# Last stage of a four-stage transformer kernel: the experts' choice compared through DRAM in place of TensorE products, and three moves of VectorE work

## The chip, the cores and the metric

The kernel runs on one core of a Trainium2 chip. The core has TensorE (matmuls), VectorE (elementwise work, reductions, 32x32 transposes), ScalarE (activation functions), GpSimd (called POOL in the profile) and SyncE (SP), which here issues nearly all DMAs. The engines run their own instruction streams and wait for each other through semaphores. The metric is the device time of the whole program in microseconds; lower is better. All data are float32.

## The reference, cut to what matters

Four residual blocks follow one another on x of shape (16, 256, 256). The change is in the fourth, a gated linear attention (GLA) with a dense branch and four sparse experts:

```
q1, k1, v = x @ Wq, x @ Wk, x @ Wv                    # 8 heads of 64
q2 = x @ Wqa @ Wqb
k2 = softmax(x @ Wka @ Wkb) over each head
gk1, gk2 = log_sigmoid(x @ Wg?a @ Wg?b + bg?) / 16
e = softmax(x @ We)                                    # 4 experts per token
mask = one_hot(top_1(e)); rw = e * mask
o_dense  = chunk_gla(q1, k1, v, gk1)
o_sparse = sum over experts of chunk_gla(q2 * rw, k2 * rw, v, gk2 * mask)
o = rmsnorm(o_dense + o_sparse) * silu(x @ Wga @ Wgb)
out = x + tanh(g) * (o @ Wo)
```

Since each token has one expert, the sum over experts needs two things only for every pair of tokens (s, t): whether they chose the same expert, and, if so, the product of their two weights. The first masks the cumulated gates, the second masks the scores of the sparse branch.

## The kernel before, in words

The program has four stages. The last one, `stage3_fast` (line 1619), is a generator: its first parts, for batch 0, run between parts of stage 2, then its own loop runs over p = 0 to 63: 16 batches of four steps, each step one pair of heads (m = p % 4). Batch 0 is prepared ahead of the loop; inside the loop, the preparation of batch b + 1 is spread over the four steps of batch b.

The order is written out by hand. The objects `dve3`, `act3` and `pool3`, and the wrappers `matmul` and `transpose`, keep program order on their engine, so each engine works through its instructions exactly in the order in which the loop calls the functions. What happens once a batch hangs in small tables (`start`, `middle`, `rest`, `late`, `behind_mask`, `by_rows`, `logs`, lines 2036 to 2045), each a point within the step; `{1: [(route, 1)]}` means: in the second step of a batch, do `route` for the next batch. I call p % 4 = 0, 1, 2, 3 the first to fourth step.

One step p does, in this order: `masked(p - 1, 1)` (scores of the sparse branch times the masks, on VectorE, out of the two-bank PSUM tile `sc`; POOL then adds both branches in `at`); `keys_queries(p + 1)` (tile `kq`); `decays(p + 1)` (matmuls of the gates with the masks, tiles `gq` and `gz`, the second with `em`, and ScalarE's exponentials `ee`); `products(p, 0)` and `masked(p, 0)`; `factors(p + 1)` (`f`); the values of the step before, tile `o`; `second` and `factors_second` (`k`, `q`); `products(p, 1)`. There is one `sc` tile, so each set of products waits until VectorE has read the set before. Small PSUM results share two banks, given out by `bank`.

Work once a batch that the change and the prediction touch:

- `lows` (1695, first step): low-rank projections, tile `low`; the four expert logits are four of its rows, so tokens lie along the free dimension.
- `route_rows` (1712), called from `products` in the first step: two TensorE transposes bring the logits to 128 token partitions.
- `route_logits` (1718), `route_sums` (1732), `route` (1737): softmax, maximum, first maximum on 128x2x4 tiles; the result is the one-hot row times its weight, tile `hot`.
- `turn_hot` (1782), `turned_hot` (1788): two TensorE transposes and a copy give `hT`, 4 experts x 256 tokens. `pairs` (1792): two matmuls of `hT` with itself, tile `both`, give for each pair the product of the weights, zero where the experts differ. VectorE makes `em` (a zero or one pattern times the causal mask) and `am` (the product times the score mask).
- `steepest` (1778): a maximum over the gates for the final range check, 128x1024, twice.
- `all_gates` (1758, second step): gate projections; two of its four results go into the `sc` tile, two into small banks.
- `outgates` (1811, first step): output gate into two small banks; ScalarE takes an exponential `eg` of each, VectorE copies each to `zs`. `outgates_end` (1825): logarithm and exponential, then POOL multiplies to `gw`.
- `turn_ahead` (1685, third step, behind `masked`): VectorE transposes the 32x32 blocks of the normalised rows of batch b + 2, 16 DMAs of 16 KB put the blocks in place (`xnT<-turned`).
- `norms` (1985, second step): ScalarE writes 8 KB to DRAM (`rms<-rs`), and two DMAs read it back spread over 64 partitions each (`r<-rms`).

SyncE issues its DMAs in order too, and a DMA that waits holds up those behind it.

Of the kernel before, what the change touches and what calls it, by code (L numbers as in the profile page):

```python
# [17 lines left out]
P = 128  # L18
# [55 lines left out]
def layers(ctx: ExitStack, tc: tile.TileContext, t, out, check):  # L74
# [1544 lines left out]
    def stage3_fast(early_bank):  # L1619

        with ExitStack() as sx:
# [29 lines left out]
            hots = [w1.tile([P, 2, 4], F32, tag=f"hot{n}", name=f"hot{n}") for n in range(2)]  # L1651
# [43 lines left out]
            def lows(b):  # L1695
# [8 lines left out]
                dve3.tensor_scalar(low[b][:, 1, :], ps[:, S:], vec[:, V_ONE:V_ONE + 1], None, ALU.add)  # L1704
                lowd[b] = of(b).tile([P, S], F32, tag="lowd", name="lowd")
# [4 lines left out]
            e_, den_, z_ = {}, {}, {}  # L1710

            def route_rows(b, ps):

                for i in range(2):
                    transpose(ps[:, 64 * i:64 * i + 64], low[b][64:P, 1, tokens(i)], ident[64:P, 64:P])
                z_["rt"] = ps

            def route_logits(b):

                ps = z_.pop("rt")  # L1720
                src = ps.rearrange("p (i e) -> p i e", i=2)[:, :, 17:21]
                mx = st.tile([P, 2], F32, tag="emx", name="emx")
                dve.tensor_reduce(mx, src, AX.X, ALU.max)
                e = e_[b] = st.tile([P, 2, 4], F32, tag="e", name="e")
                dve.tensor_tensor(e, src, bc(mx, [P, 2, 4], 2), ALU.subtract)
                act.activation(e, e, AF.Exp)

            def route_first(b):
                route_rows(b, bank("rt")[:, :P])
                route_logits(b)  # L1730

            def route_sums(b):
                den = den_[b] = st.tile([P, 2], F32, tag="eden", name="eden")
                dve.tensor_reduce(den, e_[b], AX.X, ALU.add)
                dve.reciprocal(den, den)

            def route(b):
                e, shape = e_.pop(b), [P, 2, 4]
                dve.tensor_tensor(e, e, bc(den_.pop(b), shape, 2), ALU.mult)
                m, q, c = (st.tile(x, F32, tag=n, name=n) for n, x in (("em", [P, 2]), ("eq", shape), ("ec", [P, 2])))  # L1740
                dve.tensor_reduce(m, e, AX.X, ALU.max)
                first = bc(prio[:, 4:], shape, 1)
                dve.tensor_tensor(q, e, bc(m, shape, 2), ALU.is_equal)
                dve.tensor_tensor(q, q, first, ALU.mult)
                dve.tensor_reduce(c, q, AX.X, ALU.max)
                dve.tensor_tensor(q, q, bc(c, shape, 2), ALU.is_equal)
                dve.tensor_tensor(hots[b % 2], q, e, ALU.mult)
# [34 lines left out]
            def turn_hot(b):  # L1782
                ps = bank("hT")
                for i in range(2):
                    transpose(ps[:4, tokens(i)], hots[b % 2][:, i, :], ident)
                z_[b, "hot"] = ps

            def turned_hot(b):
                hT[b] = of(b).tile([4, S], F32, tag="hT", name="hT")
                dve3.tensor_copy(hT[b], z_.pop((b, "hot"))[:4, :S])  # L1790

            def pairs(b):

                x, both = hT.pop(b), bank("both")
                matmul(both[:, 0:S], x[:, :P], x, start=True, stop=True)
                matmul(both[:, S:3 * P], x[:, P:], x[:, P:], start=True, stop=True)
                em[b] = of(b).tile([P, 2, P], F32, tag="em", name="em")
                dve3.scalar_tensor_tensor(em[b], both.rearrange("p (i s) -> p i s", i=2)[:, :, :P], 0.0, dmask,
                                          ALU.is_gt, ALU.mult)
                am[b] = of(b).tile([P, 384], F32, tag="am", name="am")  # L1800
                dve3.tensor_tensor(am[b], both[:, :384], amask, ALU.mult)
# [9 lines left out]
            def outgates(b):  # L1811
# [7 lines left out]
                for h, ps in enumerate(two):  # L1819
                    e, zs = (w2.tile([P, 512], F32, tag=n, name=n) for n in ("eg", "zs"))  # L1820
                    act3.activation(e, ps, AF.Exp, scale=-1.0)
                    dve3.tensor_copy(zs, ps)
                    z_[b, h] = zs, e
# [82 lines left out]
            def products(p, n):  # L1906
# [4 lines left out]
                if n == 0 and m == 0 and b + 1 < B:  # L1911
                    route_rows(b + 1, ps[:, 1, 384:])
# [121 lines left out]


            start = {3: [(pairs, 1)]}
            middle = {0: [(lows, 1)], 1: [(all_gates, 1)], 2: [(turn_hot, 1)], 3: [(scaled_first, 0)]}

            rest = {0: [(bias, 2)], 2: [(turned_hot, 1), (norm_ahead, 2)], 3: [(steepest, 1, 0), (steepest, 1, 1)]}
            late = {1: [(norms, -1)], 2: [(vals, 1)], 3: [(project, -1)]}  # L2040
            behind_mask = {0: [(route_logits, 1)], 2: [(turn_ahead, 2)]}
            by_rows = {0: [(outgates, 0)], 1: [(gates_end, 1)]}
            logs = {0: [(route_sums, 1), (outgates_end, 0, 0)],
# [11 lines left out]
            for group in (((bias, 0), (stats, 0)), ((norm, 0),), ((turn, 0),), ((lows, 0),), ((gates, 0, 0),),  # L2055
                          ((gate_logs, 0, 0), (route_first, 0)), ((route_sums, 0), (gates, 0, 1)),
# [6 lines left out]
            for f, *a in ((turn_hot, 0), (turned_hot, 0), (stats, 1), (pairs, 0), (norm, 1), (steepest, 0, 0),  # L2063
                          (steepest, 0, 1)):
                f(*a)
# [185 lines left out]
```

## Time and profile before

| | us |
|---|---|
| median of 3 runs (lowest, highest) | 1831.25 (1830.49, 1833.01) |
| the profiled execution: time, span from first to last instruction | 1833.27, 1831.5 |
| TensorE busy (PE), weight loads (PEld) | 1793.7 (98%), 1242.3 (68%) |
| VectorE (DVE), ScalarE (ACT), GpSimd (POOL) busy | 1137.3 (62%), 832.2 (45%), 1015.0 (55%) |
| first instruction of the last stage for batch 0 on TensorE (`low`) | at 1201.6 |

The profile names a group of instructions by engine, line, operation and out<-in of the program's tiles. Nearly all instructions of the last stage stand at a few lines, those of the helpers (L50 for VectorE, ScalarE and POOL, L1637 for matmuls, L1640 for transposes), so the tile names tell them apart. A wait is put down to what released it: "PE sc <- DVE at" is TensorE waiting, before it writes `sc`, for VectorE's instruction that writes `at`.

### The profile page before, as it was taken

Reading aid. Unit: us, or ns where it says so; the run is one execution under the profiler, and the core shown is the slowest. Engines: PE = TensorE matmul, PEld = TensorE weight load, DVE = VectorE, ACT = ScalarE, POOL = GpSimd, SP = SyncE. Lnnn points to the kernel's source line nnn. Section 1 sums busy time; section 2 is a strip of 40 time slices with the busy share of each in tenths; the row PEclk is TensorE's granted clock in tenths of the full one; section 3 lists DMA queues with packets and bytes.
Section 4 is the critical chain, followed back from the end, with each engine's and each line's share of the span. In section 5 each row is a group of like instructions: output and inputs, shape, how many; then the busy total and the mean of one; then the engine's idle time right before and its main releaser. Section 6 shows DMA issues by size and latency. Waiting matters only on the chain.

```text
span 1831.5 us, 35425 instructions
## 1 busy us (share of the span) xinstructions
PE 1793.7 (98%) x13930; PEld 1242.3 (68%) x13930; DVE 1137.3 (62%) x2695; ACT 832.2 (45%) x1727; POOL 1015.0 (55%) x1001
## 2 busy tenths in 40 slices
PE   8999999999999999999999999998999999999997
PEld 5666666666666666666777866656777777777775
DVE  3345656666656666666475388866666666666664
ACT  4433335343443334534343388754544454445432
POOL 3654766567666677656643866313454445444533
PEclk9999999999999999999999999999999999999999
DMA  9800010000010100000067933100111111111110
GB/s 303 231 1 22 16 35 13 28 17 16 31 35 10 30 20 10 28 24 17 13 207 244 256 64 50 24 3 11 35 30 36 29 31 34 34 31 27 38 31 26
DMA packets 110361, 98.05 MB, mean 54 GB/s; under 512 B 43835, under 2 KB 97763, under 8 KB 109673
## 3 DMA queue, kind: packets, MB, share of 16 engines
q1 hardware_dynamic: 97897, 78.91, 14.5%
q0 software_dynamic: 12288, 16.79, 4.5%
q8 instruction: 112, 1.84, 0.4%
q14 instruction: 64, 0.52, 0.1%
HBM read 52.03 MB, written 38.41 MB: 49 GB/s over the span
## 4 chain that ended last, share of the span: by engine, by line
PE 81%; DVE 7%; POOL 7%; ACT 2%; issue 2%; DMA 1%; SPq 0%; POOLq 0%; DVEq 0%; ACTq 0%
PE o L50 12%; PE qk L50 11%; PE v L50 9%; PE sc L50 8%; PE proj L50 7%; PE sc L1637 5%; PE kq L1637 5%; POOL es L50 4%; PE gq L1637 3%; PE v L1637 3%; PE proj L1637 3%; PE ex L50 3%; DVE at L50 2%; PE o L1637 2%; POOL rs L50 2%
## 5 line engine op out<-in xcount | busy, mean ns | idle before, releaser
L50 POOL TENSOR_SCALAR rs<-mv 128x2 f32<-128x2 f32 (+2 forms) x85 | 16.3, 191 | 398.3 <-DVE mv L50 396.5
L50 DVE RECIPROCAL rd<-o 128x256 f32<-128x256 f32 x64 | 112.3, 1755 | 155.9 <-PE o L50 155.9
L50 ACT ACTIVATE e<-sc 128x1024 f32<-128x1024 f32 (+1 forms) x192 | 181.6, 1016 | 18.4 <-PE sc L50 18.4
L50 POOL TENSOR_TENSOR at<-at,at 128x768 f32<-128x768 f32 x63 | 114.2, 1812 | 133.5 <-DVE at L50 133.5
L50 PE MATMUL sc<-qk 64*128 64x256 f32 (+1 forms) x1536 | 183.1, 384 | 0.5 <-DVE qk L50 0.5
L50 PE MATMUL o<-e,v 128*32 128x256 f32 (+1 forms) x3072 | 177.9, 379 | 0.0
L50 PEld LDWEIGHTS sc<-qk 64*128 64x128 f32 (+1 forms) x1536 | 132.0, 172 | 55.1 <-issue 26.8
L50 POOL TENSOR_TENSOR esum<-esum,es 128x512 f32<-128x512 f32 x128 | 163.4, 1277 | 10.0
L50 PE MATMUL qk<-kvT,wkv 128*128 128x333 f32 x512 | 164.3, 443 | 0.0
L50 POOL TENSOR_TENSOR es<-e 128x1024 f32<-128x1024 f32 x64 | 151.3, 2364 | 12.0 <-ACT e L50 9.0
L50 ACT ACTIVATE qk<-qk 128x256 f32<-128x256 f32 x128 | 48.8, 382 | 231.7 <-PE qk L50 231.7
L50 POOL TENSOR_TENSOR es<-es,e 77x1024 f32<-77x1024 f32 x64 | 150.3, 2349 | 5.0
L50 DVE TENSOR_TENSOR at<-sc,amask 128x768 f32<-128x768 f32 x64 | 61.3, 958 | 135.1 <-PE sc L1637 79.6
L50 PEld LDWEIGHTS o<-e,v 128*32 128x32 f32 (+1 forms) x3072 | 99.9, 110 | 66.2
L50 PE MATMUL qk<-kvT,wq 128*128 128x256 f32 x512 | 134.6, 385 | 0.0
L50 DVE COPY qk<-qk 128x333 f32<-128x333 f32 x128 | 64.6, 505 | 94.8 <-ACT qk L50 93.3
L50 POOL DMA_INDIRECT x<-rows_out,pos x64 | 100.9, 1577 | 35.8 <-issue 18.7
L50 PEld LDWEIGHTS qk<-kvT,wq 128*128 128x128 f32 x512 | 94.3, 189 | 35.1 <-issue 9.6
L50 PEld LDWEIGHTS qk<-kvT,wkv 128*128 128x128 f32 x512 | 97.2, 190 | 30.0
L50 PE MATMUL proj<-wo0h,oT 128*128 128x256 f32 x512 | 113.7, 380 | 0.3 <-DVE oT L50 0.3
L50 PE MATMUL v<-wkv,kvT 128*128 128x512 f32 x256 | 113.1, 595 | 0.0
L50 PEld LDWEIGHTS proj<-wo0h,oT 128*128 128x128 f32 x512 | 95.9, 190 | 13.9 <-issue 0.8
(267 smaller groups left out, 3919.5 us busy)
## 6 DMA issues: line engine op xcount, KB each, us to landing
rows<-zero SPq DMA_DIRECT2D x16, 640.0 KB
xin<-rows SPq DMA_DIRECT2D x16, 640.0 KB
r<-rms SPq DMA_DIRECT2D x30, 256.0 KB
rows_out<-y SPq DMA_DIRECT2D x16, 384.0 KB
v<-vctx SPq DMA_DIRECT2D x15, 308.0 KB
x<-in_x_dram SPq DMA_DIRECT2D x16, 256.0 KB
rows_out<-y SPq DMA_DIRECT2D x16, 256.0 KB
out_dram<-x SPq DMA_DIRECT2D x15, 256.0 KB
```

The lines of the kernel that those rows point to most:

```text
L50: x = getattr(self.engine, name)(*a, **k)
L1637: tc.keep_in_program_order(nc.tensor.matmul(*a, **k))
```

## The change

The experts' choice no longer goes through TensorE.

- `lows` gains a VectorE transpose of 32 rows x 256 tokens, so that the logits lie on 32 partitions, 8 blocks of tokens, 4 experts. `route_rows`, `route_first`, `turn_hot`, `turned_hot` and `pairs` are gone. `route_logits` and `route_sums` do the same arithmetic on 32 partitions with 8x4 values each.
- `route` ends with the weight `w` and the priority number `c` of the chosen expert, one of each per token, in the tile `choice`, a 32x32 transpose to `chosen`, and three DMAs on SyncE: 2 KB to DRAM (`picks`), that read back to all 128 partitions (`rows`, 256 KB, in a buffer of the tag `zs`, or for batch 0 of the tag `xn`), and read back with the tokens on the partitions (`cols_`, 128x2x2, in single 4-byte values).
- `same` (fourth step, first thing) makes `em` by comparing rows with columns, one instruction per half. `weights` (fourth step, behind `steepest`) makes `am` with four instructions: compare and multiply by the row weight, then multiply by the column weight and the mask.
- `outgates` takes the exponential and the VectorE copy of the first bank only; the second bank's exponential and copy, by `outgates_exp`, come later in the step, and the copy is made by ScalarE.
- `route_sums` moves from the end of the first step to behind `masked(p - 1, 1)` in the second.
- `turn_ahead` moves from behind `masked(p, 0)` of the third step to ahead of it, behind `vals`.
- Before the loop, batch 0 gets `steepest`, then `same` and `weights`, then `norm(1)`.

```diff
@@ -1648,7 +1648,8 @@
             low2 = w1.tile([64, P], F32, tag="low2", name="low2")
             wo = w1.tile([P, 4, D], F32, tag="wo", name="wo")
 
-            hots = [w1.tile([P, 2, 4], F32, tag=f"hot{n}", name=f"hot{n}") for n in range(2)]
+            choice, chosen = (w1.tile([P, 32], F32, tag=n, name=n) for n in ("choice", "chosen"))
+            nc.gpsimd.memset(choice, 0.0)
 
             xn, xnT, low, lg, hT, em, am, lowd = {}, {}, {}, {}, {}, {}, {}, {}
             v, gw, u_, oT = {}, {}, {}, {}
@@ -1702,49 +1703,50 @@
                                          start=k == 0, stop=k == 1)
                 dve3.tensor_copy(low[b][:, 0, :], ps[:, :S])
                 dve3.tensor_scalar(low[b][:, 1, :], ps[:, S:], vec[:, V_ONE:V_ONE + 1], None, ALU.add)
+                rl[b] = w1.tile([P, 4, P], F32, tag="turned", name="rl")[:, :2, :].rearrange("p x d -> p (x d)")
+                dve3.transpose(rl[b][64:96, :], ps[64:96, S:])
                 lowd[b] = of(b).tile([P, S], F32, tag="lowd", name="lowd")
                 nc.sync.dma_start(out=lowd[b][64:], in_=low[b][:64, 1, :])
                 if b > 0:
                     nc.sync.dma_start(out=low2, in_=low[b][64:, 1, P:])
 
-            e_, den_, z_ = {}, {}, {}
-
-            def route_rows(b, ps):
-
-                for i in range(2):
-                    transpose(ps[:, 64 * i:64 * i + 64], low[b][64:P, 1, tokens(i)], ident[64:P, 64:P])
-                z_["rt"] = ps
+            e_, den_, z_, rl, rows, cols_ = {}, {}, {}, {}, {}, {}
+            picks = [tc.dram_tile([2, S], F32, name=f"picks{b}") for b in range(B)]
+            few, own_rows = [32, 8, 4], slice(64, 96)
+
+            def small(name, shape):
+                return w1.tile([P] + shape[1:], F32, tag=name, name=name)[own_rows]
 
             def route_logits(b):
 
-                ps = z_.pop("rt")
-                src = ps.rearrange("p (i e) -> p i e", i=2)[:, :, 17:21]
-                mx = st.tile([P, 2], F32, tag="emx", name="emx")
+                src = rl.pop(b)[own_rows].rearrange("p (k c) -> p k c", c=32)[:, :, 17:21]
+                mx = small("emx", few[:2])
                 dve.tensor_reduce(mx, src, AX.X, ALU.max)
-                e = e_[b] = st.tile([P, 2, 4], F32, tag="e", name="e")
-                dve.tensor_tensor(e, src, bc(mx, [P, 2, 4], 2), ALU.subtract)
+                e = e_[b] = small("e", few)
+                dve.tensor_tensor(e, src, bc(mx, few, 2), ALU.subtract)
                 act.activation(e, e, AF.Exp)
 
-            def route_first(b):
-                route_rows(b, bank("rt")[:, :P])
-                route_logits(b)
-
             def route_sums(b):
-                den = den_[b] = st.tile([P, 2], F32, tag="eden", name="eden")
+                den = den_[b] = small("eden", few[:2])
                 dve.tensor_reduce(den, e_[b], AX.X, ALU.add)
                 dve.reciprocal(den, den)
 
             def route(b):
-                e, shape = e_.pop(b), [P, 2, 4]
-                dve.tensor_tensor(e, e, bc(den_.pop(b), shape, 2), ALU.mult)
-                m, q, c = (st.tile(x, F32, tag=n, name=n) for n, x in (("em", [P, 2]), ("eq", shape), ("ec", [P, 2])))
-                dve.tensor_reduce(m, e, AX.X, ALU.max)
-                first = bc(prio[:, 4:], shape, 1)
-                dve.tensor_tensor(q, e, bc(m, shape, 2), ALU.is_equal)
-                dve.tensor_tensor(q, q, first, ALU.mult)
+
+                e, q = e_.pop(b), small("eq", few)
+                w, c = choice[own_rows, :8], choice[own_rows, 8:16]
+                dve.tensor_tensor(e, e, bc(den_.pop(b), few, 2), ALU.mult)
+                dve.tensor_reduce(w, e, AX.X, ALU.max)
+                dve.tensor_tensor(q, e, bc(w, few, 2), ALU.is_equal)
+                dve.tensor_tensor(q, q, bc(prio[own_rows, 4:], few, 1), ALU.mult)
                 dve.tensor_reduce(c, q, AX.X, ALU.max)
-                dve.tensor_tensor(q, q, bc(c, shape, 2), ALU.is_equal)
-                dve.tensor_tensor(hots[b % 2], q, e, ALU.mult)
+                dve.transpose(chosen[own_rows], choice[own_rows])
+                nc.sync.dma_start(out=picks[b].rearrange("n (k a) -> (n k) a", a=32), in_=chosen[64:80])
+                x = w2.tile([P, 512], F32, tag="zs", name="rows") if b else w0.tile([P, 2, D], F32, tag="xn", name="rows")
+                rows[b] = x.rearrange("p (n s) -> p n s", n=2) if b else x
+                nc.sync.dma_start(out=rows[b], in_=bc(picks[b], [P, 2, S], 0))
+                cols_[b] = w1.tile([P, 2, 2], F32, tag="cols", name="cols")
+                nc.sync.dma_start(out=cols_[b], in_=picks[b].rearrange("n (i p) -> p n i", p=P))
 
             def gates(b, i):
 
@@ -1779,26 +1781,22 @@
                 dve3.tensor_reduce(check["gates"][:, 2 * b + i:2 * b + i + 1],
                                         lg[b][:, i].rearrange("p n f -> p (n f)"), AX.X, ALU.max)
 
-            def turn_hot(b):
-                ps = bank("hT")
+            def same(b):
+
+                em[b] = of(b).tile([P, 2, P], F32, tag="em", name="em")
                 for i in range(2):
-                    transpose(ps[:4, tokens(i)], hots[b % 2][:, i, :], ident)
-                z_[b, "hot"] = ps
-
-            def turned_hot(b):
-                hT[b] = of(b).tile([4, S], F32, tag="hT", name="hT")
-                dve3.tensor_copy(hT[b], z_.pop((b, "hot"))[:4, :S])
-
-            def pairs(b):
-
-                x, both = hT.pop(b), bank("both")
-                matmul(both[:, 0:S], x[:, :P], x, start=True, stop=True)
-                matmul(both[:, S:3 * P], x[:, P:], x[:, P:], start=True, stop=True)
-                em[b] = of(b).tile([P, 2, P], F32, tag="em", name="em")
-                dve3.scalar_tensor_tensor(em[b], both.rearrange("p (i s) -> p i s", i=2)[:, :, :P], 0.0, dmask,
-                                          ALU.is_gt, ALU.mult)
-                am[b] = of(b).tile([P, 384], F32, tag="am", name="am")
-                dve3.tensor_tensor(am[b], both[:, :384], amask, ALU.mult)
+                    dve3.scalar_tensor_tensor(em[b][:, i, :], rows[b][:, 1, tokens(i)], cols_[b][:, 1, i:i + 1],
+                                               dmask[:, i, :], ALU.is_equal, ALU.mult)
+
+            def weights(b):
+
+                w, c = (rows[b][:, n, :] for n in range(2))
+                x = am[b] = of(b).tile([P, 384], F32, tag="am", name="am")
+                for i, (lo, hi) in enumerate(((0, S), (S, 3 * P))):
+                    dve3.scalar_tensor_tensor(x[:, lo:hi], c[:, i * P:], cols_[b][:, 1, i:i + 1], w[:, i * P:],
+                                               ALU.is_equal, ALU.mult)
+                    dve3.scalar_tensor_tensor(x[:, lo:hi], x[:, lo:hi], cols_[b][:, 0, i:i + 1], amask[:, lo:hi],
+                                               ALU.mult, ALU.mult)
 
             def vals(b):
                 v[b] = of(b).tile([P, 2, 512], F32, tag="v", name="v")
@@ -1818,9 +1816,14 @@
                         matmul(two[h][:, i * S:(i + 1) * S], w[:, m * P:(m + 1) * P], x, start=True, stop=True)
                 for h, ps in enumerate(two):
                     e, zs = (w2.tile([P, 512], F32, tag=n, name=n) for n in ("eg", "zs"))
-                    act3.activation(e, ps, AF.Exp, scale=-1.0)
-                    dve3.tensor_copy(zs, ps)
-                    z_[b, h] = zs, e
+                    z_[b, h] = zs, e, ps
+                outgates_exp(b, 0, dve3.tensor_copy)
+
+            def outgates_exp(b, h, copy):
+                zs, e, ps = z_[b, h]
+                act3.activation(e, ps, AF.Exp, scale=-1.0)
+                copy(zs, ps)
+                z_[b, h] = zs, e
 
             def outgates_end(b, h):
                 zs, e = z_.pop((b, h))
@@ -1908,8 +1911,6 @@
                 b, m, cols = place(p)
                 q, k = fq.pop((p, n)), fk.pop((p, n))
                 ps = psa.tile([P, 2, 512], F32, tag="sc", name="sc")
-                if n == 0 and m == 0 and b + 1 < B:
-                    route_rows(b + 1, ps[:, 1, 384:])
                 for lo, hi, i in ((0, S, 0), (P, S, 1)):
                     for j in range(2):
                         r = slice(64 * j, 64 * j + 64)
@@ -2033,14 +2034,14 @@
                     matmul(ps, ones, v[B - 1][:, 0, :], start=True, stop=True)
 
 
-            start = {3: [(pairs, 1)]}
-            middle = {0: [(lows, 1)], 1: [(all_gates, 1)], 2: [(turn_hot, 1)], 3: [(scaled_first, 0)]}
-
-            rest = {0: [(bias, 2)], 2: [(turned_hot, 1), (norm_ahead, 2)], 3: [(steepest, 1, 0), (steepest, 1, 1)]}
-            late = {1: [(norms, -1)], 2: [(vals, 1)], 3: [(project, -1)]}
-            behind_mask = {0: [(route_logits, 1)], 2: [(turn_ahead, 2)]}
+            start = {3: [(same, 1)]}
+            middle = {0: [(lows, 1)], 1: [(all_gates, 1)], 3: [(scaled_first, 0)]}
+
+            rest = {0: [(bias, 2)], 1: [(route_sums, 1)], 2: [(norm_ahead, 2)], 3: [(steepest, 1, 0), (steepest, 1, 1), (weights, 1)]}
+            late = {1: [(norms, -1)], 2: [(vals, 1), (turn_ahead, 2)], 3: [(project, -1)]}
+            behind_mask = {0: [(route_logits, 1)]}
             by_rows = {0: [(outgates, 0)], 1: [(gates_end, 1)]}
-            logs = {0: [(route_sums, 1), (outgates_end, 0, 0)],
+            logs = {0: [(outgates_exp, 0, 1, act3.copy), (outgates_end, 0, 0)],
                     1: [(route, 1), (stats, 2), (outgates_end, 0, 1), (gate_logs, 1, 0)],
                     2: [(gate_logs, 1, 1), (normed_out, -1, 0), (normed_out, -1, 1)]}
 
@@ -2053,15 +2054,14 @@
                 x.tied = True
             yield
             for group in (((bias, 0), (stats, 0)), ((norm, 0),), ((turn, 0),), ((lows, 0),), ((gates, 0, 0),),
-                          ((gate_logs, 0, 0), (route_first, 0)), ((route_sums, 0), (gates, 0, 1)),
+                          ((gate_logs, 0, 0), (route_logits, 0)), ((route_sums, 0), (gates, 0, 1)),
                           ((route, 0), (vals, 0), (gate_logs, 0, 1), (bias, 1))):
                 for f, *a in group:
                     f(*a)
                 yield
             psu = sx.enter_context(tc.tile_pool(name="f3psu", bufs=1, space=PSUM, side="right", reuse_waits="tile"))
             keys_queries(0)
-            for f, *a in ((turn_hot, 0), (turned_hot, 0), (stats, 1), (pairs, 0), (norm, 1), (steepest, 0, 0),
-                          (steepest, 0, 1)):
+            for f, *a in ((stats, 1), (steepest, 0, 0), (steepest, 0, 1), (same, 0), (weights, 0), (norm, 1)):
                 f(*a)
             yield
             w1 = sx.enter_context(tc.tile_pool(name="f3w1", bufs=1, reuse_waits="tile"))
```

## The prediction

> **What bounds the kernel now.** The change lies in the last stage, so I first cut the span into windows of 37 us, about one batch of that stage, then read who waits for whom in it, then the chain of waits inside one batch. A line of the windows view gives start:end and length, busy us (and instructions) of PE, PEld, DVE, ACT, POOL, then clock, DMA share and GB/s:
>
> ```profile
> 1499.00:1536.00 37.00, 36.53 (x254) 26.89 (x252) 24.25 (x60) 17.75 (x43) 17.68 (x18) 1.00 0.13 32
> ```
>
> TensorE is busy 36.5 of 37 us at full clock; VectorE, the next, 24.3. Every window from 1277 to 1758 reads alike, so the stage runs at the pace of TensorE. Two views say what else it spends. The waits of PE over the stage (total, times, longest):
>
> ```profile
> PE sc L1637 <- DVE at L50: 7.7, 16, 1.0
> PE low L1637 <- DMA xnT<-turned: 1.7, 1, 1.7
> PE sc L1637 <- ACT lg L50: 0.6, 1, 0.6
> PE o L1637 <- POOL at L50: 0.5, 1, 0.5
> ```
>
> and the chain of waits through one batch (start, us, what):
>
> ```profile
> 1509.62 0.22 PE hT L1640 x2
> ...
> 1517.11 0.84 PE both L1637 x4
> ...
> 1532.30 0.28 PE sc L1640
> ...
> 1535.44 1.29 DVE zs L50 x2
> 1536.73 0.33 DVE q L50
> 1537.06 0.08 DVE eden L50
> 1537.14 0.02 issue
> 1537.16 0.17 DVE eden L50
> 1537.33 1.30 DVE at L50 x4
> 1538.63 0.04 issue
> 1538.67 0.70 PE sc L1637 x2
> ```
>
> The batch repeats every 36.76 us (1501.91, then 1538.67). The last lines are the one place where TensorE stands still in each batch: `all_gates` takes the score bank that `masked` reads, and waits 0.46 us for it.
>
> **TensorE work removed**, in 15 of 16 batches (batch 0 is prepared before the loop). `turn_hot`: 0.22 us by the chain, and its neighbours follow without a gap. `pairs`: 0.84; the check is that from the first score matmul before it to the next `kq` is 1.60 us here and 0.75 one step earlier, where nothing stands between. `route_rows`: the chain says 0.28, but from the end of the matmuls before to the start of those behind the scores is 0.78 us with it and 0.78 and 0.79 in the third and fourth steps without it. Its two 64-column transposes seem to run in half of the array beside the scores, so it is worth between 0 and 0.28; I take 0.1, near the equal intervals. Sum 1.16 us, times 15 = **17.4 us**.
>
> **The 0.46 us wait.** Ahead of the four `at` instructions that release the bank, VectorE loses the second gate copy (1.29 us for two, so 0.64) and `route_sums` (q to at, 0.27): it is ready 0.91 us earlier, while TensorE arrives only 0.1 earlier. VectorE's added 0.44 us transpose in `lows` (row: the 128x256 transpose `dens`, 439 ns) falls between 1532.25 and the scores at 1533.3, where it idles 1.21 us. What is late next: the second gate bank, now freed by ScalarE. Its order becomes Exp, Square 0.60, Exp 0.38, Exp 0.58, copy (row: `v` copy, 592 ns); from 1534.9 that ends near 1537.5, and TensorE wants the bank at 1538.15. The wait goes: 14 x 0.45 + 1.0 (the first) = **7.3 us**. The price is on POOL: ScalarE's Ln and Exp (1.28) end near 1538.8, not 1537.83, so `gw` (1.27) and the sum of `at` (1.81) end at 1541.9, and TensorE now reaches the values at 1541.8: 0.1 a batch, **1.5 us back**; between 0 and 0.5 a batch, as the ScalarE order packs. Moved `route_sums` lies in 3.28 us of VectorE idle behind the masking.
>
> **VectorE in the fourth step of a batch** is the tightest place. Gone: `em` 0.425, `am` 0.547, and the 0.70 transpose of `turn_ahead`, which moves one step of the order up into 3.78 us of idle before 1515.14. So q ends at 1517.03, not 1517.63. Added: two 128-column selections (row: `at<-sc,kden,am`, 341 ns at 128 columns, 472 at 256; in a row they cost 0.08 less each) 0.6 us; four in `weights` 2 x 0.47 + 2 x 0.34 = 1.6. Line: selections to 1517.58, at to 1518.88, gating to 1519.48, the two maxima (2.33) to 1521.73, weights to 1523.3. The projection, without the 0.84 of `pairs`, is ready at 1523.43. It fits with 0.1 us to spare, so cost 0; SBUF operands could make the six shorter, dependent pairs longer, and 0.5 us over would be 7 us in all. `route` has six small instructions of 0.16 to 0.2 us for seven. In the first batch no projection covers the masks, so VectorE runs late there: about 2.0 us lost, and against it the only wait for xnT, 1.7 + 0.2 us with its weight load, goes because the turned rows leave 3.5 us sooner. Net 0.1.
>
> **The new transfers.** The added wait is `same`, for rows and cols; behind it on VectorE stand the masking, the gating and all of the fourth step. Nearest rows, in SyncE's part of the timeline:
>
> ```profile
> 1506.67 0.61 SPq L1995 DMA_DIRECT2D rms<-rs  x1
> ...
> 1508.42 1.32 SPq L1998 DMA_DIRECT2D r<-rms  x2
> ...
> 1516.79 10.33 SPq L1693 DMA_DIRECT2D xnT<-turned  x16
> ```
>
> This is the same round trip by DRAM: the read starts 1.75 us after the write. SyncE is free from 1509.74 until the turned rows. Choice is ready at 1508.7, so picks go at 1509.74, rows at 1511.5 to 1512.1, cols to 1512.7; the turned rows, ready at 1513.2, lose nothing. From end of issue to landing: in the first batch the turned rows were issued until 1270.58 and their reader ran at 1272.12, 1.54 us; r's 512 KB took about 1.1 us more, so I give the 256 KB of rows 0.6. Rows land near 1514.3, cols near the same; `same` wants them at 1516.8 (TensorE being 0.22 ahead). Hidden, 2.5 us of cover.
>
> Here a rule speaks against the change. cols is 512 pieces of 4 bytes. The Trainium skill, DMA: Bandwidth & Descriptors, "Rules for kernel authors", says that a non-contiguous last dimension becomes one descriptor per element and should be rearranged; its "Specifications" ask for 512 bytes a piece. The trace has no such transfer; the nearest, turned rows in 128 pieces of 128 bytes, are issued in 0.6 us each. By the row cols costs 0.6 + 1.54; by the rule, with issue growing with the number of pieces, 2.4 + 1.54, landing at 1516.1 and pushing the turned rows 1.3 us. By both it is hidden: sum 0 either way, and only the cover shrinks to 0.7. I take the row.
>
> **Before the loop** the round trip of batch 0 starts at 1220.1 and lands near 1225.5. But `same` and `weights` now stand behind the two maxima (2.34) on VectorE: em is done at 1227.3, where `gz` started at 1226.38. **0.9 us lost**, up to 3 if the transfers are late.
>
> **Sum:** 17.4 + 7.3 - 1.5 - 0.1 - 0.9 = 22.2 us from the profiled execution's 1833.27 (span 1831.5 and 1.8 around it): 1811.1. That execution lay 2.0 above the median of 1831.25, so I predict **1809 us**. Best end: route_rows 0.28, no POOL wait, no loss early: 1803. Worst of the hidden costs (POOL 0.5, VectorE 0.5 a batch, 3 us early): 1809 + 6 + 7 + 2 = 1824.
>
> **Rivals.** *VectorE or POOL become the wait* (15 in 100): the selections or the order gw, at cost 0.5 us in each batch: 1816. For it: 0.1 us of slack at both. Against: both busy under two thirds of the batch. *The transfers land late* (14 in 100, slower): one mechanism, cols' 512 pieces, 32 to each of 16 DMA engines. All behind `same` waits, TensorE with it at the score bank. The gain is 1.5 us a batch, so it decides when cols land 6.3 us after their issue begins, not 2.1: 4.2 us for 32 pieces, 130 ns each. The page's mean packet on this queue is 0.145 x 1831.5 x 16 / 97897 = 43 ns, which speaks against; no row with such small pieces speaks for nothing worse. At 165 ns: 2.7 us late, 15 x 2.7 = 40, time 1849. *Partly late* (7): 1 to 1.6 us a batch, 1824 to 1833. *It doesn't shorten the path*, because something else holds the pace: VectorE at 24.8 us of 35.2 (plus 2.75, less 2.23) and ScalarE at 18.3 leave that to little (2).
>
> **Chances.** Forecast 62, the small waits 15, partly late 7, no effect 2, late 14. Under 0.2% (3.7 us) a measurement of this kernel can't tell a change. Faster 0.82, same 0.04, slower 0.14. Range 1801 to 1826: it leaves out the late transfers and a little of partly late.
>
> **What would show it.** A batch period near 35.2 us; no PE wait for `at` in the second step; hT and both gone; PE still busy over 98% of a window; `same` with no wait for a DMA; the `x<-proj` idle of 1.24 us nearly gone. I am wrong if `same` idles for cols, if `o` waits for POOL by more than 0.3 us, or if the score matmuls of the fourth step wait for `at`.

## The result, and the profile after

| | us | ratio to before (95% interval) |
|---|---|---|
| before, run again beside it: median of 8 (lowest, highest) | 1832.88 (1830.49, 1836.09) | |
| after: median of 8 (lowest, highest) | 1840.61 (1837.06, 1844.89) | 1.0046 (1.0034 to 1.0059) |
| after, the profiled execution: time, span | 1839.75, 1838.0 | |

The change makes the kernel 0.5% slower. The forecast was 1809, with a range from 1801 to 1826.

TensorE did lose work. Engine totals of the page of after (busy us, share of the span, instructions):

```profile
PE 1779.9 (97%) x13802; PEld 1228.7 (67%) x13802; DVE 1157.9 (63%) x2727; ACT 843.6 (46%) x1743; POOL 1015.8 (55%) x1002
```

PE is busy 13.8 us less than before (1793.7), in a span 6.5 us longer. So some 20 us of standing still are new. The windows view of after, for the same 37 us as before (columns as in the prediction):

```profile
1499.00:1536.00 37.00, 35.20 (x240) 25.40 (x238) 25.10 (x61) 18.17 (x42) 17.15 (x19) 1.00 0.17 39
```

TensorE works 35.2 of 37 us, at full clock, where it worked 36.5. The waits of the stage, all engines, after (who waited for whom: total us, times, longest):

```profile
DVE em L50 <- DMA cols<-picks: 37.8, 15, 3.2
...
PE sc L1637 <- DVE at L50: 15.8, 16, 1.9
...
PE gz L1637 <- DVE em L50: 12.5, 14, 2.4
```

The first line is the new wait: VectorE, at `em` in `same`, waits 15 times for the transfer of the columns, 2.5 us a time. It is the prediction's own sign of being wrong, "`same` idles for cols". The other two are what TensorE pays for it: at `gz`, which multiplies by `em`, and at the score bank, which VectorE reads only after `em`. Before, `gz` had no such line and `sc` had 7.7 us. Why the columns are late is seen in SyncE's part of the timeline of after, one batch (start, length, us):

```profile
1508.16 0.61 SPq L1996 DMA_DIRECT2D rms<-rs  x1
...
1509.91 1.31 SPq L1999 DMA_DIRECT2D r<-rms  x2
...
1511.31 0.55 SPq L1744 DMA_DIRECT2D picks<-chosen  x1
...
1515.14 1.95 SPq L1694 DMA_DIRECT2D xnT<-turned  x3
...
1517.20 0.52 SPq L1747 DMA_DIRECT2D rows<-picks  x1
...
1517.76 0.43 SPq L1749 DMA_DIRECT2D cols<-picks  x1
...
1518.24 8.32 SPq L1694 DMA_DIRECT2D xnT<-turned  x13
```

In the text of the kernel, `route` issues rows and cols in the second step and `turn_ahead` its 16 DMAs in the third. On the queue, three of the 16 stand ahead of rows; why the compiled order has them there is not shown. They wait for VectorE's transpose, which ends at 1515.07, then take 1.95 us to issue, and rows and cols wait behind them. The chain of waits of after through that place (start, length, what):

```profile
1516.49 0.59 SPq L1694
1517.09 0.05 issue
1517.14 0.03 SPq L1747
1517.17 0.03 issue
1517.20 0.52 SPq L1747
1517.72 0.04 issue
1517.76 3.35 DMA cols<-picks
...
1521.21 0.35 DVE em L50
...
1521.86 1.39 DVE at L50 x4
...
1528.32 0.87 DVE at L50
1529.20 0.04 issue
1529.24 0.92 PE sc L1637 x8
```

The chain that sets the end of the batch now runs through SyncE's queue and VectorE; before, it ran through TensorE nearly all the way. From the start of `em` to the score matmuls VectorE has no slack, so what the transfer is late comes out at TensorE.

The batch can be measured from one `low` matmul to the next. I use it below, since it is free of what the earlier stages do: the median over the batches from the third interval on is **36.76 us before and 37.47 after**.

### The profile page after: what moved, and what is told of

Its sections match the earlier page's. It is cut to its first block, busy times and chain, and to the rows that moved or that the text cites. A ratio compares the mean times of both kernels' runs of the same rounds, so it can differ in the third digit from the quotient of the medians.

```text
span 1838.0 us, 35247 instructions
## 1 busy us (share of the span) xinstructions
PE 1779.9 (97%) x13802; PEld 1228.7 (67%) x13802; DVE 1157.9 (63%) x2727; ACT 843.6 (46%) x1743; POOL 1015.8 (55%) x1002
## 4 chain that ended last, share of the span: by engine, by line
PE 68%; DVE 11%; POOL 9%; issue 4%; DMA 3%; ACT 2%; SPq 1%; POOLq 0%; DVEq 0%; ACTq 0%
PE o L50 11%; PE qk L50 11%; PE v L50 9%; PE sc L50 8%; PE proj L50 7%; POOL es L50 4%; PE kq L1637 3%; PE ex L50 3%; DVE at L50 3%; PE v L1637 3%; DMA cols<-picks 3%; PE sc L1637 2%; DVE gates L50 2%; POOL rs L50 2%; PE low L1637 2%
## 5 line engine op out<-in xcount | busy, mean ns | idle before, releaser
L50 PEld LDWEIGHTS qk<-kvT,wq 128*128 128x128 f32 x512 | 94.3, 189 | 35.2 <-issue 9.6
```

What stands on the lines that cost most here:

```text
L50: x = getattr(self.engine, name)(*a, **k)
```

## The experiments

Theory 1, after the traces: the order on SyncE's queue holds rows and cols back. Against it: the transfers themselves are slow (`picks` waits behind `r`'s 512 KB, or the 4-byte pieces of cols take long), or VectorE's new work is the cost, whatever SyncE does. The diffs are against after unless it says otherwise; "..." marks what is left out. The results of all ten:

| kernel | median us | ratio to before (95%) | batch, us |
|---|---|---|---|
| after | 1840.6 | 1.0046 (1.0034 to 1.0059) | 37.47 |
| order tied | 1813.0 | 0.9886 (0.9868 to 0.9904) | 35.42 |
| turn_ahead at its old place | 1819.4 | 0.9923 (0.9907 to 0.9938) | 35.94 |
| the three moves alone | 1820.6 | 0.9930 (0.9913 to 0.9946) | 36.23 |
| the DRAM choice alone | 1835.7 | 1.0015 (1.0008 to 1.0023) | 37.01 |
| order tied, picks ahead of r | 1810.8 | 0.9892 (0.9877 to 0.9907) | 35.34 |
| order tied, cols copied | 1812.3 | 0.9898 (0.9883 to 0.9913) | 35.36 |
| both of these | 1812.3 | 0.9907 (0.9891 to 0.9922) | 35.36 |
| order tied, gate copy on VectorE | 1824.0 | 0.9966 (0.9952 to 0.9979) | 36.14 |
| after's order by hand, picks ahead of r | 1839.2 | 1.0045 (1.0031 to 1.0059) | 37.43 |
| after's order by hand, cols copied | 1834.3 | 1.0011 (1.0004 to 1.0018) | 36.98 |

The ratio is to the kernel before, run beside each group: its median was 1833.1 beside the four kernels below after, 1829.7 beside the next four and 1832.3 beside the last two. Medians of different groups can therefore differ by some 3 us for that alone.

### The order of the text, tied

Rows, cols and the 16 turned DMAs keep the order in which the program calls them. Nothing else differs.

```diff
-                        nc.sync.dma_start(out=to[r:r + 32, :, q:q + 32], in_=y[q:q + 32, :, r:r + 32])
+                        tc.keep_in_program_order(nc.sync.dma_start(out=to[r:r + 32, :, q:q + 32], in_=y[q:q + 32, :, r:r + 32]))
...
-                nc.sync.dma_start(out=rows[b], in_=bc(picks[b], [P, 2, S], 0))
+                tc.keep_in_program_order(nc.sync.dma_start(out=rows[b], in_=bc(picks[b], [P, 2, S], 0)))
...
-                nc.sync.dma_start(out=cols_[b], in_=picks[b].rearrange("n (i p) -> p n i", p=P))
+                tc.keep_in_program_order(nc.sync.dma_start(out=cols_[b], in_=picks[b].rearrange("n (i p) -> p n i", p=P)))
```

> The changed kernel with one thing added: rows, cols and the sixteen turned-row DMAs keep the order of the program on SyncE, so rows and cols go out ahead of all turned rows. Theory 1 (queue order): three turned-row DMAs stood ahead of rows on SyncE, and rows went out 4 us late; with the order restored rows issue 1.8 us after picks, cols land about 3 us after their issue, em waits for no DMA, the PE waits for em (12.5 us) and most of those for at (15.8 us) go, and the time is 1810 to 1816. Theory 2 (the 512 pieces of cols land late by themselves, or are slowed by the turned rows behind them): em still waits 1.5 us or more a batch, 1825 to 1840. Theory 3 (VectorE is over-full in the fourth step even without the DMA wait): em waits for no DMA but PE still waits about 1 us a batch for at, 1824 to 1828.

1813.0 us: 27.6 below after and 1.1% below before. The timeline of this kernel, SyncE and `em` in one batch:

```profile
1502.57 0.34 SPq L1747 DMA_DIRECT2D rows<-picks  x1
...
1502.96 0.43 SPq L1749 DMA_DIRECT2D cols<-picks  x1
...
1503.49 10.34 SPq L1694 DMA_DIRECT2D xnT<-turned  x16
...
1506.38 0.74 DVE L50 SCALAR_TENSOR_TENSOR em<-rows,cols,dmask 128x128 f32<-128x128 f32 x2 [0.57 <-DMA cols<-picks]
...
1513.41 0.95 DVE L50 TENSOR_TENSOR at<-sc,amask 128x768 f32<-128x768 f32 x1
...
1514.41 0.92 PE L1637 MATMUL sc<-q,k 64*128 64x256 f32 x8
```

`em` still waits for cols, 0.57 us in place of 2.74, against the expectation of no wait. The score matmuls of the fourth step start 0.05 us after `at` and have no idle time recorded ahead of them. TensorE's waits in this kernel:

```profile
PE sc L1637 <- DVE at L50: 5.4, 7, 1.9
PE gz L1637 <- DVE em L50: 3.1, 2, 2.4
```

The two waits fall by 10.4 and 9.4 us against after, 19.8 of the 25.3 us between the spans (1838.0 and 1812.7). Some 2 us of the rest show as longer groups: behind the wait, the four `gz` matmuls of after take 0.75 us in twelve batches and 0.87 in one, where they take 0.61 without one. Theory 1 is shown: the same instructions, in another order on one DMA queue, are worth 27.6 us.

### turn_ahead at its old place

```diff
-            late = {1: [(norms, -1)], 2: [(vals, 1), (turn_ahead, 2)], 3: [(project, -1)]}
-            behind_mask = {0: [(route_logits, 1)]}
+            late = {1: [(norms, -1)], 2: [(vals, 1)], 3: [(project, -1)]}
+            behind_mask = {0: [(route_logits, 1)], 2: [(turn_ahead, 2)]}
```

> The changed kernel with turn_ahead back behind the masking of the third step, everything else as changed. Theory 1: the turned rows are ready only after rows and cols are out, so the order is right without any pin, em waits for no DMA; VectorE's 0.7 us transpose is again ahead of the fourth step's work, so the masks there are some 0.4 us late: 1815 to 1822. Theory 2: em waits for cols as before, 1835 or more. Theory 3: em without wait, and PE waits for at 1.5 us a batch or more, 1828 to 1835.

1819.4 us, with nothing tied: from the old place the turned DMAs fall behind rows and cols by themselves (rows at 1507.34, turned at 1510.61). So it is this move that put three of them ahead in after. Against the tied kernel, which has turn_ahead at the new place, this one is 6.4 us slower, so the move itself is worth having: TensorE's `kq <- f` (3.3 us, 14 times) and `low` (3.5 us for xnT and its issue), both absent in the tied kernel, are where its loss shows.

### The three moves without the DRAM choice

The kernel before, with only `route_sums`, `turn_ahead` and the gate copy moved; its pair products stay.

```diff
-            rest = {0: [(bias, 2)], 2: [(turned_hot, 1), (norm_ahead, 2)], 3: [(steepest, 1, 0), (steepest, 1, 1)]}
-            late = {1: [(norms, -1)], 2: [(vals, 1)], 3: [(project, -1)]}
-            behind_mask = {0: [(route_logits, 1)], 2: [(turn_ahead, 2)]}
+            rest = {0: [(bias, 2)], 1: [(route_sums, 1)], 2: [(turned_hot, 1), (norm_ahead, 2)], 3: [(steepest, 1, 0), (steepest, 1, 1)]}
+            late = {1: [(norms, -1)], 2: [(vals, 1), (turn_ahead, 2)], 3: [(project, -1)]}
+            behind_mask = {0: [(route_logits, 1)]}
...
-            logs = {0: [(route_sums, 1), (outgates_end, 0, 0)],
+            logs = {0: [(outgates_exp, 0, 1, act3.copy), (outgates_end, 0, 0)],
```

> The kernel before with the three moves alone (second gate copy by ScalarE, route_sums behind the masking, turn_ahead ahead of the masking), the choice still by pair products on TensorE. The forecast's 0.46 us wait for the score bank in the second step goes (7 us), the one wait for xnT too (2 us), against 0.1 us a batch for POOL: 1823 to 1828 beside 1833. A rival that the moves give nothing because POOL's later sum of at takes the wait over: 1830 to 1834.

1820.6, better than the 1823 to 1828 expected. The batch takes 36.23 us against 36.76, so the three moves are worth 0.53 each batch: the 0.46 us wait at the score bank, which is gone, and a little more. The second interval falls from 36.24 to 33.54: the turned rows leave earlier, and the one 1.7 us wait for xnT goes with them, as does a 1.0 us wait for the score bank. The prediction set a loss of 2.0 us, from the late masks of the first batch, against the gain at xnT. That loss did come in after. The score matmuls of the fourth step in the first batch, before and after:

```profile
1267.03 0.92 PE L1637 MATMUL sc<-q,k 64*128 64x256 f32 x8 [0.32 <-DVE at L50]
...
1267.03 0.92 PE L1637 MATMUL sc<-q,k 64*128 64x256 f32 x8 [1.88 <-DVE at L50]
```

The wait is 1.56 us longer in after; in the kernel of the three moves it is 0.31 us, as before. The second interval of after is as short as here (33.66) because the choice's matmuls have left it as well.

### The DRAM choice without the three moves

```diff
-                outgates_exp(b, 0, dve3.tensor_copy)
...
+                    dve3.tensor_copy(zs, ps)
...
-            logs = {0: [(outgates_exp, 0, 1, act3.copy), (outgates_end, 0, 0)],
+            logs = {0: [(route_sums, 1), (outgates_end, 0, 0)],
```

> The changed kernel with the three moves undone: the choice by DRAM alone. Theory 1: rows go out ahead of the turned rows, PE loses 17 us of products, keeps the 0.46 us wait of the second step and gets 0.4 to 1 us a batch of waiting for at in the fourth: 1820 to 1830. Theory 2: em waits for cols, 1840 or more. Theory 3: 1832 to 1840 by waits for at alone.

1835.7: theory 1's 1820 to 1830 is missed. Rows are ahead of the turned rows here, and still nothing is won. The timeline of this kernel at `all_gates`, second step:

```profile
1504.85 0.70 PE L1637 MATMUL sc<-lbg,low 17*128 17x512 f32 x2 [1.07 <-DVE at L50]
```

The wait for the score bank is 1.07 us where it was 0.46. Both sides moved: counted from the first `low` matmul, TensorE arrives 0.14 us earlier than before (8.58 against 8.72), and VectorE frees the bank 0.48 us later (9.60 against 9.12), since VectorE takes 5.78 us and not 5.17 from the start of that step's first `at` to the end of the one that frees the bank. In after, where the second gate copy and `route_sums` have left this stretch, it is 4.62. The other losses of this kernel are `kq <- f` (3.3 us in all) and further waits for `at` (21.2 us in all, of which some 15 are the 14 of 1.07). The parts do not add: moves alone -12.5 us, DRAM choice alone +2.6, both with the order tied -20.1.

### picks ahead of r's reads

The tied kernel, with `picks` issued between `norms`' write and its two reads, and rows and cols behind those.

```diff
...
-                    1: [(route, 1), (stats, 2), (outgates_end, 0, 1), (gate_logs, 1, 0)],
+                    1: [(route, 1), (norms_read, -1), (spread, 1), (stats, 2), (outgates_end, 0, 1), (gate_logs, 1, 0)],
```

> The pinned kernel with picks issued ahead of the two r<-rms reads on SyncE, not behind them. In the pinned kernel rows went out 3.9 us after picks, not the 1.75 us that the write and read of rms take. Theory A: picks, 2 KB, waits in the DMA engines behind the 512 KB that r's two reads put there just before; ahead of them it lands in under 2 us, and rows go out right behind r, about 1.5 us sooner measured from the time chosen is ready. Theory B: the write of picks is slow by itself (16 pieces of 128 bytes): rows still wait 3.5 us or more behind picks. Time by either: em's wait of 0.6 to 0.8 us a batch was mostly covered, so 1809 to 1814.

SyncE in the timeline of this kernel:

```profile
1499.00 0.33 SPq L1744 DMA_DIRECT2D picks<-chosen  x1
...
1499.44 1.32 SPq L2005 DMA_DIRECT2D r<-rms  x2
...
1500.86 0.54 SPq L1749 DMA_DIRECT2D rows<-picks  x1
...
1501.45 0.42 SPq L1751 DMA_DIRECT2D cols<-picks  x1
```

From picks to rows it is 1.86 us, and 3.90 in the tied kernel, where r's 512 KB went ahead (1498.67 to 1502.57; medians 1.88 and 3.86). So that part of the rival is true. `em` no longer waits, but for 0.3 us once, before the loop. But the time, 1810.8, can't be told from the tied kernel's (ratios 0.9892 and 0.9886). The timeline of this kernel shows what took the place of the wait:

```profile
1505.27 2.50 POOL L50 TENSOR_TENSOR u<-u,r 128x512 f32<-128x512 f32 x2
...
1506.82 1.37 DVE L50 SCALAR_TENSOR_TENSOR em<-rows,cols,dmask 128x128 f32<-128x128 f32 x2
...
1515.16 0.38 PE L1637 MATMUL gz<-low,lbk 64*128 64x256 f32 x1
1515.48 0.92 PE L1637 MATMUL sc<-q,k 64*128 64x256 f32 x8
```

The pair of `em` instructions, 0.61 to 0.74 us in after, now takes 1.37: the first lasts 1.10 us instead of some 0.35. In each of the 14 batches from the third on, the pair ends 0.40 to 0.42 us after POOL's `u<-u,r`, whatever its length, here and in the kernel with both changes below. So an `em` that starts early appears to be held until that POOL work is done. This is read from the traces alone: no run changes that POOL work, and how it holds `em` is not shown. Counted from the end of `q`, `em` ends after 1.29 us here and 1.32 in the tied kernel (medians), and the cover that was won is worth nothing. In both, VectorE stays late to the end of the fourth step: the score matmuls start 0.32 us behind the start of the `gz` matmul ahead of them (median; 0.40 tied) and take 0.92, and before they did so in 0.21 and took 0.82.

### cols by copies, and both together

Four ScalarE copies of the choice, 32 partitions each, in place of the DMA with 4-byte pieces: on the tied kernel, then on the one above.

```diff
...
-                nc.sync.dma_start(out=cols_[b], in_=picks[b].rearrange("n (i p) -> p n i", p=P))
+                x = choice[own_rows, :16].rearrange("p (n i q) -> p n i q", n=2, i=2)
+                for q in range(4):
+                    act3.copy(cols_[b][32 * q:32 * q + 32], x[:, :, :, q])
```

> The pinned kernel with cols made by four copies of ScalarE from the tile choice (32 partitions each, behind the gates' logarithms) in place of the DMA of 512 pieces of 4 bytes. If the pieces are slow (cols landed 3.0 us after the end of its issue, the turned rows 1.54), em waits for no DMA now, since rows lands first: its idle of 11.4 us in all falls under 3. If all DMAs land 3 us after their issue at that place, em waits for rows instead, by about the same. Time 1809 to 1813; a rival by ScalarE's 0.8 us of added copies ahead of the normalisation: 1814 to 1820.

> Both of these on the pinned kernel: picks ahead of r, cols by copies. No DMA wait left at em, a batch period of 35.2 to 35.4 us, 1807 to 1812; not measurably better than either alone if the wait at em was covered on TensorE all along.

1812.3 and 1812.3, neither apart from the tied kernel; the second lies 0.3 above its expected range. With cols copied and picks behind r, `em` still waits for rows, 4.6 us in 6 batches: the 256 KB broadcast lands 3.05 us after the end of its issue (median), the small pieces in the tied kernel 3.0 after theirs. With both changes no wait for a DMA is left.

### The gate copy back on VectorE

```diff
-            logs = {0: [(outgates_exp, 0, 1, act3.copy), (outgates_end, 0, 0)],
+            logs = {0: [(outgates_exp, 0, 1, dve3.tensor_copy), (outgates_end, 0, 0)],
```

> The pinned kernel with the second gate copy on VectorE again, at its new place in the order. By the forecast's reading of the second step (VectorE's at releases the score bank just as TensorE comes), 0.7 us more ahead of at makes TensorE wait 0.5 to 0.9 us in each batch: 1820 to 1828. If something else holds the second step, 1812 to 1815.

1824.0, 11 us slower than the tied kernel by the medians, and 0.72 a batch, which is 10.8 in 15 (by the two ratios it would be 15). At `all_gates` in its timeline:

```profile
1495.90 0.70 PE L1637 MATMUL sc<-lbg,low 17*128 17x512 f32 x2 [0.84 <-DVE at L50]
```

The second copy takes VectorE 0.69 us ahead of `at`, behind 0.23 us of idle for ScalarE's exponential, and TensorE waits for it in each batch, 0.84 us in this one. With the DRAM choice in place, ScalarE's copy is worth more than the 0.46 us that the wait was before.

### after's queue, rebuilt by hand

Two kernels put rows (and cols) behind the third turned DMA by hand, and then take away one other suspect each: the first has picks ahead of r's reads, the second has cols by copies.

```diff
...
+                        if b > 2 and (q, r) == (0, 96):
+                            spread(b - 1)
...
```

> The changed kernel's order of SyncE, three turned-row DMAs ahead of rows, written out by hand, with picks alone moved ahead of r's reads. If rows is held by the three turned rows, which wait for VectorE, then an earlier picks helps nothing: rows goes out as before behind them, em waits for cols as in the changed kernel, 1836 to 1844. If the late landing of picks behind r were the cause, em's wait would fall by 2 us a batch: 1812 to 1820.

> The changed kernel's order of SyncE, three turned-row DMAs ahead of rows, with cols made by ScalarE's copies and no cols DMA. Rows goes out as late as in the changed kernel, but is the last to land: if the 512 pieces cost 1 to 1.5 us of landing, em's wait falls from 2.7 us a batch to 1.2 to 1.7, and with PE's waits 1 to 1.4 us a batch the time to 1819 to 1827. If rows lands as late as cols did, no change: 1836 to 1844.

The first: 1839.2, no better than after. SyncE in its timeline:

```profile
1510.85 0.33 SPq L1746 DMA_DIRECT2D picks<-chosen  x1
...
1511.29 1.30 SPq L2011 DMA_DIRECT2D r<-rms  x2
...
1515.41 1.95 SPq L1696 DMA_DIRECT2D xnT<-turned  x3
...
1517.47 0.52 SPq L1755 DMA_DIRECT2D rows<-picks  x1
```

picks now goes out ahead of r's reads, 6.62 us before rows where it was 5.88, and rows is issued as late as ever: the three turned DMAs hold the queue until 1517.4. Against the kernel with picks first, only the place of rows and cols differs, and it costs 28.4 us. The second: 1834.3, between the two ranges that were expected, 4.9 us below the first. `em` there waits for rows, 30.2 us in 13 batches or 2.3 a time, against 2.7. Those 0.4 us are the place in the queue and not the pieces: cols is issued behind rows, 0.43 us and a gap of 0.04, and from the end of its issue it lands no later than rows does from its own (3.0 us in after, 3.05 here).

## Where the prediction was right and where wrong

**The step that failed is "The new transfers".** It put rows at 1511.5, behind picks at 1509.74, on the ground that SyncE is free until the turned rows. It counted the instructions that SyncE gets but took their order from the text. Three of its terms were wrong:

- *The order.* The move of `turn_ahead`, which the prediction costed on VectorE alone, brought three of its DMAs ahead of rows. From picks to rows the forecast was 1.75 us; it is 3.86 with the order tied and 5.88 in after (medians), so the order adds 2.0, which is the 1.95 us that the three take to issue. Tying the order takes back 27.6 us; rebuilding after's order brings the time back to 1839.2. This is the cause.
- *The landing of picks.* The other 2.1 us from picks to rows. 1.75 us, taken from `rms` to `r`, was the right row only for a write with nothing large ahead of it: 1.36 us before the loop, 1.88 or less ahead of r's reads, 3.86 behind them.
- *The landing of rows and cols.* Forecast from the end of the issue: 0.6 + 1.54 us for rows and 1.54 for cols, with 1.54 from the turned rows, which stay in SBUF. Measured 3.0 for both (medians of 2.95 to 3.05 in the kernels in which `em` waits in most batches). Rows and cols come from DRAM; that this is the reason is not shown by a run. The prediction's own reading of r's 512 KB from DRAM, 1.54 + 1.1 us, would have been nearer. The Trainium skill, DMA: Bandwidth & Descriptors, "Anatomy of one DMA — SWDGE (gpsimd) path", fits some 2.0 us and the bytes at 436 GB/s for one DMA of GpSimd's path; for the 262144 bytes of rows that gives an estimate of 2.6 us, nearer to the measured 3.0, on SyncE's queue, than the row that I took. For the 2 KB of cols it gives 2.0, and cols took 3.0 too.

Together 2.0 + 2.1 + 1.5 us, less 0.2 for shorter issues: 5.4 us, which ate the 2.5 us of cover and nearly 3 more; `em` waits 2.74 in the median batch of after. Without the order's 2.0 some 0.9 would be left, and the tied kernel waits 0.6.

**The rival "the transfers land late"** had the place right (`em`, behind it the masks, then TensorE at the score bank) and the cause wrong: it needed 130 ns for each 4-byte piece. cols is issued in 0.43 us, no longer than other DMAs, and lands no later after its issue than the broadcast of rows. Of the prediction's two prices for cols, 0.6 + 1.54 by the row and 2.4 + 1.54 by the rule against a non-contiguous last dimension, neither fits the measured 0.43 + 3.0: the issue did not grow with the pieces, and the landing was too short in both.

**The other terms, most of which held.** The tied kernel has the order of SyncE that the prediction assumed, and the one with picks first also its short way from picks to rows; their profiled spans, 1812.7 and 1811.2 against 1831.5, are 18.8 and 20.3 us of the 22.2 forecast, and both times lie in its range. Term by term:

- *TensorE's work:* 17.4 us forecast; PE busy is 1777.0 in the tied kernel, 16.7 less than before.
- *A batch:* 1.16 + 0.45 - 0.1 = 1.51 us forecast; 36.76 - 35.34 = 1.42 measured with picks first. In part this is luck, for two misses cancel. `route_rows` was worth 0.21 us a batch, not 0.1: from the start of `gz` to that of `o` in the first step it is 2.47 us before and 2.26 in every kernel without it. The 0.78 us that the prediction compared came from steps with other matmuls between. And VectorE cost about 0.2, as the next but one says.
- *The score bank in the second step:* the wait is gone in after and in the tied kernel, as said, but for 0.52 us in the first batch. It goes by little: VectorE frees the bank 0.75 us earlier than before and TensorE comes 0.28 earlier (0.91 and 0.1 forecast), which leaves 0.07 us to spare. The price on POOL, 0.1 us a batch, came out near 0.15 (from the score matmuls of that place to `o`, 1.01 us against 0.86).
- *VectorE in the fourth step:* here the forecast of no cost did not hold. The selections took 0.35 to 0.48 us each, as taken, all but the first of `em` with picks first (1.10), but `em` was done 1.3 us behind `q`, not 0.6: it waited for cols in the tied kernel and lasted until POOL's `u<-u,r` was done in the one with picks first. The score matmuls are 0.1 to 0.2 us late for it and 0.1 longer, an estimate of 3 to 4.5 us in 15 batches from the medians above. Whether the step fits where nothing holds `em`, no run shows.
- *The first batches:* a net loss of 0.1 us forecast. The loss from the late masks came, 1.56 us of the 2.0, and the wait for xnT went; with the removed matmuls the second interval became 2.6 us shorter (36.24 to 33.67). The first interval became 1.1 longer in the tied kernel and 0.3 shorter in after, and nearly all of the difference is the clock that TensorE was granted. Up to the first `gz<-em` the three agree within 0.05 us (24.80, 24.75, 24.75); from there to the second `low` it is 9.50 us at a granted clock of 0.72 and then 0.57 before, 9.23 at 0.63 in after, 10.65 at 0.50 and then 0.56 in the tied kernel. What moves the clock there stays open.
- *Before the loop:* 0.9 us of loss forecast. From the `kq` matmuls to `gz` it is 4.10 us before (1222.28 to 1226.38) and 4.76 after (1222.63 to 1227.39), with 2.43 us of it a wait for `em` where hT and the pair products were: 0.66 lost.

## What to carry to other kernels

A moved step moves its DMAs too, and on a queue that issues in order the place that counts is that of the instruction stream, not of the text: read the order off the compiled stream or the trace, or tie it, before pricing a wait. Price a transfer by one of the same kind, a DRAM read by a DRAM read, and ask what lies ahead of it in the DMA engines. A wait that goes away wins nothing where another hold ends at the same place: look at when the instruction ends, not only at when it starts. Parts of a change that give and use the same slack are worth their sum only together: here one half alone cost 2.6 us, the other gained 12.5, and both gained 20.1.

## What was unexpected of the hardware

- A 2 KB write to DRAM completes 1.36 to 1.88 us after its issue begins with nothing large ahead, and 3.86 us behind 512 KB of reads issued just before it on the same queue. The Trainium skill, DMA: Bandwidth & Descriptors, "Queues, rings and completion order", says that all DMAs of one issuing engine use the same ring on each DMA engine, and that a completion is written only after the earlier writes of that DMA engine; the two numbers agree with that, and no run here separates the two parts.
- A DMA of 512 pieces of 4 bytes is issued in 0.43 us, a turned one of 128 pieces of 128 bytes in 0.65: issue time does not follow the number of pieces here.
- A VectorE instruction that seems to be held by POOL counts as busy: where it starts early under POOL's `u<-u,r`, the first `em` lasts 1.10 us in place of some 0.35, and the pair of them ends 0.40 to 0.42 us after that POOL work in 14 of 14 batches of two kernels. No wait is recorded.
- The four `gz` matmuls take longer right after a wait for their weights (0.75 or 0.87 against 0.61 us), so a stall of TensorE costs 0.14 us, once 0.26, more than its idle time shows. The eight `sc<-q,k` of the fourth step take 0.92 against 0.82 us with such a wait, and as long in the tied kernel, where TensorE has no idle time recorded and only its weight load waited (0.37 us for `at`).
